# Position attention, linear attention and sorted experts on one core: sorted rows turned by loads and VectorE, and four changes of order

## The chip, the core and the metric

The kernel runs on one core of a Trainium2 chip. A core has five engines that run their own instruction streams in order and wait for each other through semaphores: TensorE (PE in the profile; PEld is its loading of weights), VectorE (DVE), ScalarE (ACT), GpSimd (POOL) and SyncE (SP), which here only issues DMAs. Sixteen DMA engines move data between the chip's memory (DRAM) and the core's buffers. The metric is the time of one execution on the device, in microseconds (us), as the median of several runs. The profile is of one such execution; its span runs from the first to the last instruction.

## What is computed

The input is `x`, 4 images of 32 channels of 128 x 128 values in fp32. Two layers follow each other, image by image:

```
# layer 0: attention over the positions of 2x2 patches
q      = x as [128 (channel, r, s), 4096 positions] of an image       # 64 x 64 positions
energy[i, j] = (q[:, i] . q[:, j]) / (|q[:, i]| |q[:, j]|)            # 4096 x 4096
x      = gamma * (sum over j of softmax_j(energy)[i, j] * q[:, j]) + q

# layer 1: 4096 tokens t of 128 values (the rows of x)
t = t + linear attention(LayerNorm(t))          # 8 heads, K^T V first, then Q (K^T V)
p = softmax(LayerNorm(t) @ router_w + router_b) # 8 experts
t = t + sum over the two likeliest experts e of  p_e / (p_1 + p_2) * (LayerNorm(t) @ W_e + b_e)
```

The bulk of the work is the 4096 x 4096 energy of layer 0, cut into 8 chunks of 512 positions. It is symmetric before the softmax's division, so that a tile of exponents serves two rows of chunks.

## The kernel before

**Layer 0, `attend`.** Row `i` of 8 has the tiles `jc = 0..i`, each of four *steps* `j`. A step issues one product `pe` (line 609), its exponential `pr` on ACT (L612), and what is due from two queues. `turn_tick` (L416) runs what was queued with `after(ticks, f)`: two steps after a `pr`, its product `po` with the values (L497); one step after it, the turn of `pr` into `F` in 32 x 32 blocks on DVE (L421 in the profile, a helper's line). When a tile's four `pr` are turned, `move` stores `F` to DRAM (`blocks<-F`, L530), and three steps later `bring` loads the blocks back in exchanged places (`F<-blocks`, L545, six DMAs). This is an *F exchange*; `F` then holds the tile transposed and is used for row `jc`. That use is a *share*: four products `pg` (L433, or L453 for the diagonal tile), each with a sum on ACT (L438) and at the end an addition on DVE (L442). A share is put in the list `late` with a due time; `step_share` (L468) does one quarter of the first share in the list, if its due time has come by a counted clock:

```python
late.append((at or clock[0] + LAG, transposed_share(b, st, i, jc, G)))   # LAG = 57
```

A full step adds 8 to the clock and a quarter of a share adds 4. When row `i` has had its last `po`, ACT copies the bank out (`o<-po`, L502). There is one such bank, so the next row's first `po`, at the third step (`j == 2`) of its first tile, needs that copy.

**What runs beside it.** PE, DVE, ACT and SP follow the order in which the Python code calls them (a manual schedule); GpSimd has an order of its own. Besides `attend` of image `b` there are generators that are advanced between steps: `prep` loads and scales the next image's chunks (quarters of rows in `xa`, turned by DVE into `qT`, L316; squares and sums, L295 and L296; the power -1/2 on GpSimd, L164; `wide`, L388; `pnorm` on PE, L399), and the layer 1 of the image before (`all_parts`), one advance (`yield`) in each half of a step. For image 0 `prep_first` makes the first pair of chunks and `prep(0, 1)` the second, each with 512 KB of quarters in one and the same buffer (`xin`, tag `xx`).

**Layer 1.** `close_rows` divides, normalises and forms a Gram matrix; `matrix` folds the heads; `attention_rows(u)` for each quarter of the tokens fetches normalised rows in 128-byte pieces (`blocks<-rows`, L938), adds the attention, takes statistics (`close_stats`, whose power runs on GpSimd) and normalises again on ACT (L696). After every second quarter `sorted_experts(h)` handles half of the tokens (`h` = 0, 1). It sorts by expert: GpSimd scatters each token's row twice to `xs` in DRAM (L1066), in tiles of 128 rows that belong to one expert, 39 tiles for a half. Each row is 132 values long, 128 of the token and its weight in the rest. Then, for pairs of tiles, SP loads them (`xn<-xs`, L1096), PE turns each tile with the identity (L1137), ACT evicts the turned pair (L1106), PE multiplies each tile by its expert's matrix (L1130), DVE multiplies by the weights while it evicts (`results<-pys`, L1112), and SP stores the pair (`ys<-results`, L1116). Last, GpSimd gathers each token's two rows (L1178). Images 0 to 2 do this; the last image's experts are done densely at the end (L1304).

Of the kernel before, what the change touches and what calls it, by code (L numbers as in the profile page):

```python
# [12 lines left out]
F32 = mybir.dt.float32  # L13
# [9 lines left out]
def kernel(  # L23
# [43 lines left out]
    nc = tc.nc  # L67
# [231 lines left out]
        rows = st["T"][:, ts(kc, 8), :]  # L299
        return rows.rearrange("p k (w r) -> p k w r", r=2)  # L300

    def load_quarters(b, kc, queues=(nc.sync, nc.sync)):

        xa = xin.tile([P, 2, 2, 2, HW2, 2], F32, tag="xx", name=f"xa_{b}_{kc}")
# [7 lines left out]
        return xa  # L312

    def turn_quarters(s, xa, qT):
        for k in range(2):
            nc.vector.transpose(  # L316
                qT[:, s, 2 * k : 2 * k + 2, :].rearrange("p h (e r c) -> p r (h e) c", e=2, r=2),
                xa[:, s, k].rearrange("p r (h t) e -> p (r h) e t", h=2),
            )

    def prep_first(st):

        b, kc = 0, 0
        st["T"] = big1.tile([P, KT, D], F32, tag="T", name="T_0")
        xa = load_quarters(b, kc, (nc.sync, nc.scalar))
        qT = chunks_of(b, kc, st)
        yield
        ss = stat.tile([P, 2 * NJ], F32, tag="ss", name=f"ss_{b}_{kc}")
        rn = stat.tile([P, 2 * NJ, 1], F32, tag="rn", name=f"rn_{b}_{kc}")
        for s in range(2):  # L330
            turn_quarters(s, xa, qT)
            squares(b, kc, s, qT, ss)
            pow_neg_half(rn[:, ts(s, NJ), 0], ss[:, ts(s, NJ)])
        keep_running(40, ps_g, "pg")
        scaled = []
        for s in range(2):
            qs = work.tile([P, NJ, P], F32, tag="qs", name=f"qs_{b}_{kc}_{s}", bufs=2)
            nc.vector.tensor_tensor(qs, qT[:, s], rn[:, ts(s, NJ)].to_broadcast([P, NJ, P]), ALU.mult)
            scaled.append(qs)
        for s, qs in enumerate(scaled):  # L340
            qn = channels(b, kc, s, st)
            pt, done = hold(f"ptn_{b}_{kc}_{s}", lambda p, qn=qn: nc.scalar.activation(qn, p, AF.Copy))  # L342
            for j in range(NJ):
                nc.tensor.transpose(pt[:, ts(j, P)], qs[:, j, :], ident)
            done()
            yield

    def prep(b, kc, st):

        ahead = 2 if b == 0 and kc == 1 else 5
        xa = load_quarters(b, kc)
# [3 lines left out]
        for _ in range(ahead):  # L357
            yield
        qT = chunks_of(b, kc, st)
        for s in range(2):  # L360
# [17 lines left out]
        rn = stat.tile([P, 2 * NJ, 1], F32, tag="rn", name=f"rn_{b}_{kc}")  # L378
        for s in range(2):
            squares(b, kc, s, qT, ss)  # L380
            if s == 1:
                pow_neg_half(rn[:, :, 0], ss)
            yield
        for _ in range(ahead - 2):
            yield
        wide = work.tile([P, NJ, 2, 64], F32, tag="qs", name=f"wide_{b}_{kc}", bufs=2)
        for s in range(2):
            nc.vector.tensor_copy(wide[:, :, s], rn[:, ts(s, NJ)].to_broadcast([P, NJ, 64]))  # L388
        yield
        if b:  # L390
            yield

        def scale_all(bank):
            for s in range(2):
                scale(s, bank, lambda ap: ap.rearrange("p (j a t) -> p a j t", a=4, t=S))

        bank, done = hold(f"pnorm_{b}_{kc}", scale_all)
        for j in range(NJ):
            nc.tensor.transpose(bank[:, ts(j, P)], wide[:, j].rearrange("p s c -> p (s c)"), ident)  # L399
        yield  # L400
        done()
        yield
# [71 lines left out]
    def attend(b, st):  # L474
# [11 lines left out]
        for i in range(NCH):  # L486
# [94 lines left out]
            for jc in order:  # L581
# [21 lines left out]
                for j in range(NJ):  # L603
                    t = NJ * jc + j
                    c0 = 0 if jc < i else P * j
                    yield
                    tick[0] += 1
                    pe = ps_e.tile([P, CH], F32, tag="pe", name=f"pe_{b}_{i}_{t}")
                    nc.tensor.matmul(pe[:, c0:], qn[jc][:, ts(j, P)], qn[i][:, c0:], start=True, stop=True)  # L609
                    pr = ppool.tile([P, CH], F32, tag="pr", name=f"pr_{b}_{i}_{t}")  # L610
                    exps[:] = [
                        nc.scalar.activation(pr[:, c0:], pe[:, c0:], AF.Exp, accum_out=sums[:, t, i : i + 1]).ins  # L612
                    ]
                    own.append(pr)
                    if ending and jc == order[-1] and j == NJ - 1:
                        st["exps"] = True
                    after(2, partial(values, pr[:, c0:], t, c0, CH))
                    if jc < i and not both:
                        after(1, partial(nc.vector.transpose, Fb[:, :, :, j, :], pr))
                        if j == NJ - 1:  # L620
                            after(2, partial(move, F, i, jc))
                    elif jc == i and not ending:
                        if j < NJ - 1:
                            after(1, partial(turn_blocks, F, pr, j))
                        if j == NJ - 2:
                            after(2, partial(move_diagonal, F, i))
                    elif jc == i and j in (1, 2):

                        after(1 if j == 2 and order[-1] == i else 2, partial(below, own, (2, 1) if j == 1 else (3,)))
                    turn_tick()  # L630
                    clock[0] += 2 * (CH - c0) // P
                    step_share()
                    yield

    def finish():
# [18 lines left out]
    def layer1(b, st):  # L654
# [288 lines left out]
        def attention_rows(u):  # L943
# [17 lines left out]
            for j in range(8):  # L961
                stats[j]()
                if j == 3:
                    yield
                    yield
            logits = router_rows(nc.vector, 8 * u, 8, la)
            close_stats("f", 8 * u, 8, bs)
            next(logits)
            yield
            nc.sync.dma_start(t2[:, ts(u, 8)], T[:, ts(u, 8), :])  # L970
            yield
# [15 lines left out]
        def sorted_experts(h):  # L987
# [112 lines left out]
            def products(turned, applied):  # L1100
# [36 lines left out]
                        nc.tensor.transpose(p[:, ts(j, P)], bufs[g % 6][:, j, :D], ident)  # L1137
                return done

            if "results" not in keep:  # L1140
                keep["results"] = work.tile([P, 4, 2, D], F32, tag="df", name=f"results_{b}", bufs=1)
            done = None
            begins = []
            for at in range(len(pairs) + 5):
                if at < len(pairs):
                    load(*pairs[at])
                if done:
                    done()
                yield
                turned, applied = (pairs[at - d] if 0 <= at - d < len(pairs) else None for d in (3, 4))  # L1150
                done = products(turned, applied) if turned or applied else None
                yield
            if done:
                done()
            if h == 1:
                st["sorted"] = True
            yield from idle(1)
# [271 lines left out]
    for b in range(B):  # L1429

        if b == 0:
# [80 lines left out]
```

## Time and profile before

| | us |
|---|---|
| median of 3 runs | 1651.85 (1651.45 to 1653.72) |
| the profiled execution | 1650.83 |
| its span | 1649.0 |

| group | count | busy us | mean ns |
|---|---|---|---|
| L1137 PE pys<-ident,xn, transposes of sorted tiles | 234 | 45.2 | 273 |
| L1130 PE pys<-ew_sb,xn, their products | 468 | 71.6 | 275 |
| L1106 ACT xn<-pys, eviction of a turned pair | 120 | 45.2 | 377 |
| L1112 DVE results<-pys,xn, 128x256 | 114 | 48.2 | 423 |
| L421 DVE F<-pr, turn of 128x512 | 440 | 305.4 | 700 |
| L938 SP blocks<-rows, DMA issue | 48 | | 744 (median) |

Matmuls overlap, so that a PE group's mean is longer than the time for which one holds PE. A product in fp32 has two records, a transpose one. Letters before the arrow name what is written, those after it what is read. "Idle before" is the engine's idle time just ahead of a group, with what ended it.

### The profile page before, as it was taken

Reading aid. Unit: us, or ns where it says so; the run is one execution under the profiler, and the core shown is the slowest. Engines: PE = TensorE matmul, PEld = TensorE weight load, DVE = VectorE, ACT = ScalarE, POOL = GpSimd, SP = SyncE. Lnnn points to the kernel's source line nnn. Section 1 sums busy time; section 2 is a strip of 40 time slices with the busy share of each in tenths; the row PEclk is TensorE's granted clock in tenths of the full one; section 3 lists DMA queues with packets and bytes.
Section 4 is the critical chain, followed back from the end, with each engine's and each line's share of the span. In section 5 each row is a group of like instructions: output and inputs, shape, how many; then the busy total and the mean of one; then the engine's idle time right before and its main releaser. Section 6 shows DMA issues by size and latency. Waiting matters only on the chain.

```text
span 1649.0 us, 21309 instructions
## 1 busy us (share of the span) xinstructions
PE 1609.9 (98%) x5192; PEld 846.5 (51%) x5192; DVE 931.5 (56%) x2383; ACT 898.5 (54%) x2839; POOL 593.8 (36%) x565
## 2 busy tenths in 40 slices
PE   8999999999999999999999999999999999999987
PEld 4444544455554455555554455555554455555633
DVE  4543353567586443549478443448658634345786
ACT  3555445466475555547556455556656555545386
POOL 1000000001015441446555543256555652437166
PEclk9999999999999999999999999999999999999999
DMA  4655656676759777997899777798699877886001
GB/s 143 205 179 178 197 187 213 222 231 204 168 196 283 239 222 220 266 257 200 211 221 287 253 236 241 222 268 230 196 209 279 275 248 236 248 251 192 14 14 39
DMA packets 304297, 345.37 MB, mean 209 GB/s; under 512 B 82096, under 2 KB 230704, under 8 KB 289840
## 3 DMA queue, kind: packets, MB, share of 16 engines
q1 hardware_dynamic: 269712, 304.50, 59.9%
q0 software_dynamic: 26624, 25.58, 7.6%
q10 hardware_dynamic: 7840, 13.93, 2.9%
q8 instruction: 44, 0.72, 0.2%
q14 instruction: 77, 0.63, 0.1%
HBM read 167.08 MB, written 182.09 MB: 212 GB/s over the span
## 4 chain that ended last, share of the span: by engine, by line
PE 81%; DVE 7%; DMA 5%; ACT 3%; SPq 2%; issue 1%; POOL 1%; ACTq 0%; DVEq 0%; POOLq 0%
PE po L497 24%; PE pe L609 23%; PE pg L433 20%; PE pys L1130 3%; PE py L1304 3%; PE pg L453 2%; PE pys L1137 2%; PE pgram L725 2%; DMA F<-blocks 1%; DVE F L421 1%; DMA blocks<-rows 1%; SPq L938 1%; ACT pr L612 1%; ACT xn L696 1%; DMA blocks<-F 1%
## 5 line engine op out<-in xcount | busy, mean ns | idle before, releaser
L612 ACT ACTIVATE pr<-pe 128x512 f32<-128x512 f32 (+1 forms) x576 | 322.4, 560 | 547.5 <-PE pe L609 507.0
L497 PE MATMUL po<-pr,qT 128*128 128x512 f32 (+3 forms) x1152 | 549.4, 559 | 4.2 <-ACT o L502 3.9
L609 PE MATMUL pe<-qn,qn 128*128 128x512 f32 x896 | 458.8, 594 | 4.6 <-ACT pr L612 4.6
L433 PE MATMUL pg<-F,qT 128*128 128x512 f32 x880 | 449.8, 593 | 4.7 <-DMA F<-blocks 4.7
L421 DVE STREAM_TRANSPOSE F<-pr 128x512 f32<-128x512 f32 x440 | 305.4, 700 | 134.5 <-ACT pr L612 124.7
L497 PEld LDWEIGHTS po<-pr,qT 128*128 128x128 f32 x1152 | 215.2, 190 | 250.2 <-issue 217.9
L1178 POOL DMA_INDIRECT acc<-ys,place x128 | 202.1, 1579 | 209.1 <-ACT pr L612 134.8
L438 ACT ACTIVATE junk<-F 128x512 bf16<-128x512 f32 x440 | 273.0, 620 | 4.9 <-DMA F<-blocks 4.9
L433 PEld LDWEIGHTS pg<-F,qT 128*128 128x128 f32 x880 | 166.8, 190 | 199.4 <-issue 182.3
L1066 POOL DMA_INDIRECT xs<-xn,place x192 | 186.0, 969 | 184.1 <-ACT pr L612 118.9
L609 PEld LDWEIGHTS pe<-qn,qn 128*128 128x128 f32 x896 | 155.6, 191 | 119.1 <-issue 106.7
L442 DVE TENSOR_TENSOR o<-o,pg 128x512 f32<-128x512 f32 x110 | 75.1, 683 | 205.4 <-PE pg L433 205.2
L1112 DVE TENSOR_TENSOR results<-pys,xn 128x256 f32<-128x256 f32 x120 | 49.9, 416 | 187.2 <-ACT xn L1106 168.5
L164 POOL TENSOR_TENSOR rn<-ss,neg_half 128x8 f32<-128x8 f32 (+1 forms) x17 | 27.2, 1602 | 320.0 <-DVE ss L296 319.9
L612 ACT ACTIVATION_READ_ACCUMULATOR pr<-pe 128x1 f32 x576 | 111.9, 194 | 0.0
L1106 ACT ACTIVATE xn<-pys 128x256 f32<-128x256 f32 x120 | 45.2, 377 | 111.4 <-PE pys L1137 111.4
L1130 PEld LDWEIGHTS pys<-ew_sb,xn 128*128 128x128 f32 x468 | 70.5, 191 | 52.2 <-issue 49.7
L609 PE MATMUL pe<-qn 128*128 128x512 f32 (+3 forms) x256 | 91.4, 440 | 0.7 <-ACT qn L342 0.7
L1178 POOL DMA_INDIRECT yb<-ys,place x64 | 60.8, 950 | 81.1 <-DMA F<-blocks 31.1
L438 ACT ACTIVATION_READ_ACCUMULATOR junk<-F 128x1 f32 x440 | 84.5, 192 | 0.0
L1130 PE MATMUL pys<-ew_sb,xn 128*128 x468 | 71.6, 275 | 0.0
L1304 PE MATMUL py<-ew_sb,xn 128*128 128x512 f32 x128 | 61.5, 622 | 5.1 <-ACT tmp L1260 3.9
(217 smaller groups left out, 1463.2 us busy)
## 6 DMA issues: line engine op xcount, KB each, us to landing
blocks<-F SPq DMA_DIRECT2D x110, 1024.0 KB
F<-blocks SPq DMA_DIRECT2D x220, 192.0 KB
F<-blocks SPq DMA_DIRECT2D x220, 128.0 KB
xn<-xs SPq DMA_DIRECT2D x114, 132.0 KB
ys<-results SPq DMA_DIRECT2D x114, 128.0 KB
F<-blocks SPq DMA_DIRECT2D x220, 64.0 KB
below<-F SPq DMA_DIRECT2D x31, 384.0 KB
T<-in_x_dram SPq DMA_DIRECT2D x64, 128.0 KB
```

The costliest lines, as they stand in the source:

```text
L421: f()
L433: nc.tensor.matmul(pg.rearrange("p (a f) -> p a f", a=4), st["qT"][i][:, ib, :], G[:, :, ib], start=(ib == 0), stop=(ib == NJ - 1),)
L438: nc.scalar.activation(junk, G[:, :, ib], AF.Copy, accum_out=st["sums"][:, NJ * i + ib, jc : jc + 1])
L442: nc.vector.tensor_tensor(st["o"][jc], st["o"][jc], pg, ALU.add)
L497: nc.tensor.matmul(row["po"][:, lo:hi], qT[blk // NJ][:, blk % NJ, :], w, start=start, stop=(row["left"] == 0))
L609: nc.tensor.matmul(pe[:, c0:], qn[jc][:, ts(j, P)], qn[i][:, c0:], start=True, stop=True)
L612: nc.scalar.activation(pr[:, c0:], pe[:, c0:], AF.Exp, accum_out=sums[:, t, i : i + 1]).ins
L1066: inst = nc.gpsimd.indirect_dma_start(xs[h], offset(place[:, i, k : k + 1]), xn[:, k, :], None)
L1112: nc.vector.tensor_tensor(result[:, :n], p[:, 2 * P : 2 * P + n * D].rearrange("p (j c) -> p j c", c=D), bufs[g % 6][:, :n, D : D + 1].to_ ...
L1130: nc.tensor.matmul(p[:, 2 * P + j * D : 2 * P + j * D + D], bufs[6 + g % 2][:, j, :D], weights[:, bass.ds(begins[2 * (g % 2) + j], D)], st ...
L1178: inst = nc.gpsimd.indirect_dma_start(to, None, ys, offset(place[:, i, k : k + 1]), compute_op=op)
L1304: nc.tensor.matmul(bank, xn[:, k, :D], ew_sb[:, 4 * h : 4 * h + 4, :], start=True, stop=True)
```

## The change

Five things change.

1. In the first half (`h == 0`) of an image's sorted rows, TensorE no longer turns the tiles. Four loads for each group of up to four tiles bring 32 x 32 blocks, in rows of 128 bytes, to the places where a turn of blocks alone completes the transpose; DVE turns 128 x 512 at once; PE multiplies four tiles into one bank, and one eviction and one store serve four tiles. The weights of all rows come by one load of their own (`factor`, 39 values for each of 128 partitions). The second half stays as it was.
2. At the start of image 0, the second pair's quarters have a buffer of their own and are loaded right after the first pair's; their four turns stand between the first pair's operations on DVE.
3. In a step that is the third of a row's first tile, `step_share` comes ahead of `turn_tick`. In all steps the clock is advanced ahead of both.
4. `attention_rows` has three more `yield`s: before the logits and the statistics' end, after them, and before the store of `t2`.
5. `prep` of image 0 has one `yield` more before `pnorm`, as the other images have.

```diff
+        def rows_squared(s):
             turn_quarters(s, xa, qT)
-            squares(b, kc, s, qT, ss)
+            sq = work.tile([P, NJ, P], F32, tag="qs", name=f"sq_{b}_{kc}_{s}", bufs=2)
+            nc.vector.tensor_tensor(sq, qT[:, s], qT[:, s], ALU.mult)
+            return sq
...
+        summed(0, rows_squared(0))
+        sq = rows_squared(1)
+        st["turns"].pop(0)()
+        scale_rows(0)
+        summed(1, sq)
+        st["turns"].pop(0)()
+        st["turns"].pop(0)()
+        scale_rows(1)
+        st["turns"].pop(0)()
...
+        soon = b == 0 and kc == 1
+        if soon:
+            xa = load_quarters(b, kc, place=(work, "wide"))
+            yield
...
+        if soon:
+            st["turns"] = [partial(turn_quarter, s, k, xa, qT) for s in range(2) for k in range(2)]
+            yield
...
-        if b:
-            yield
+        yield
...
-                    turn_tick()
                     clock[0] += 2 * (CH - c0) // P
-                    step_share()
+                    steps = (turn_tick, step_share)
+                    for step in reversed(steps) if jc == order[0] and j == 2 else steps:
+                        step()
                     yield
...
+            yield
             logits = router_rows(nc.vector, 8 * u, 8, la)
             close_stats("f", 8 * u, 8, bs)
+            yield
             next(logits)
+            yield
             yield
             nc.sync.dma_start(t2[:, ts(u, 8)], T[:, ts(u, 8), :])
...
+            def load_blocks(g, n):
+                rows = xs[h][4 * g * P : (4 * g + n) * P, :D].rearrange("(m i) w -> i m w", i=S)
+                for q in range(4):
+                    read(
+                        nc.sync.dma_start(
+                            parts[g % 2][ts(q, S), : n * D].rearrange("i (m c) -> i m c", c=S), rows[:, :, ts(q, S)]
+                        )
+                    )
+
+            def turn(g, n):
+                nc.vector.transpose(parts[2 + g % 2][:, : n * D], parts[g % 2][:, : n * D])
+
+            def four_products(factor, g, n):
+
+                def leave(p):
+                    result = keep["results"].rearrange("p g j c -> p (g j) c")[:, ts(g % 2, 4)]
+                    nc.vector.tensor_tensor(
+                        result[:, :n], p[:, : n * D].rearrange("p (j c) -> p j c", c=D),
+                        factor[:, 4 * g : 4 * g + n].to_broadcast([P, n, D]), ALU.mult,
+                    )
+                    nc.sync.dma_start(
+                        ys[4 * g * P : (4 * g + n) * P, :].rearrange("(j p) d -> p j d", p=P), result[:, :n]
+                    )
...
+            def turned_by_vector():
+
+                factor = stat.tile([P, NT, 1], F32, tag="factor", name=f"factor_{b}_{h}", bufs=1)
+                read(nc.sync.dma_start(factor, xs[h].rearrange("(t p) w -> p t w", p=P)[:, :, D : D + 1]))
+                leaves = {}
+                for at in range(4 * len(quads) + 10):
+                    for first_at, act in (
+                        (8, turn), (0, load_blocks), (11, partial(four_products, factor)), (13, lambda g, n: leaves.pop(g)()),
+                    ):
+                        if at >= first_at and (at - first_at) % 4 == 0 and (at - first_at) // 4 < len(quads):
...
+            yield from (turned_by_tensor if h else turned_by_vector)()
...
     next(first)
-    load_weights()
-    next(first)
     next(second)
+    load_weights()
+    ordered.enter_context(tc.manual_schedule(engines=ENGINES))
+    next(second)
+    next(first)
     load_tokens(states[0]["T"][:, 0:8, :], 0, 0, 8)
-
-    ordered = ExitStack()
-    ordered.enter_context(tc.manual_schedule(engines=ENGINES))
-    timed = [(first, 0, 1, 2), (second, 0.5, 5.5, 10)]
+    next(second)
+    next(second)
+    timed = [(first, 0, 1, 2), (second, 1.3, 5.5, 8)]
```

More of the change, by code (lines that the diff above doesn't have):

```diff
@@ L300, in rows_of_image, with load_quarters @@
         return rows.rearrange("p k (w r) -> p k w r", r=2)
-    def load_quarters(b, kc, queues=(nc.sync, nc.sync)):
-        xa = xin.tile([P, 2, 2, 2, HW2, 2], F32, tag="xx", name=f"xa_{b}_{kc}")
+    def load_quarters(b, kc, queues=(nc.sync, nc.sync), place=(xin, "xx")):
+        xa = place[0].tile([P, 2, 2, 2, HW2, 2], F32, tag=place[1], name=f"xa_{b}_{kc}")
         halves = x[b].rearrange("c (s g) w -> c s (g w)", s=2)
@@ L312, in load_quarters, with turn_quarter @@
         return xa
+    def turn_quarter(s, k, xa, qT):
+        nc.vector.transpose(
+            qT[:, s, 2 * k : 2 * k + 2, :].rearrange("p h (e r c) -> p r (h e) c", e=2, r=2),
+            xa[:, s, k].rearrange("p r (h t) e -> p (r h) e t", h=2),
+        )
     def turn_quarters(s, xa, qT):
         for k in range(2):
[L316 to L319, printed above, removed]
+            turn_quarter(s, k, xa, qT)
     def prep_first(st):
@@ L329, in prep_first, with summed, scale_rows @@
         rn = stat.tile([P, 2 * NJ, 1], F32, tag="rn", name=f"rn_{b}_{kc}")
-        for s in range(2):
+        def rows_squared(s):
             turn_quarters(s, xa, qT)
-            squares(b, kc, s, qT, ss)
+            sq = work.tile([P, NJ, P], F32, tag="qs", name=f"sq_{b}_{kc}_{s}", bufs=2)
+            nc.vector.tensor_tensor(sq, qT[:, s], qT[:, s], ALU.mult)
+            return sq
+        def summed(s, sq):
+            nc.vector.tensor_reduce(ss[:, ts(s, NJ)], sq, AX.X, ALU.add)
             pow_neg_half(rn[:, ts(s, NJ), 0], ss[:, ts(s, NJ)])
[L334 to L337, printed above, removed]
+        def scale_rows(s):
+            qs = work.tile([P, NJ, P], F32, tag="grp", name=f"qs_{b}_{kc}_{s}", bufs=2)
             nc.vector.tensor_tensor(qs, qT[:, s], rn[:, ts(s, NJ)].to_broadcast([P, NJ, P]), ALU.mult)
             scaled.append(qs)
+        scaled = []
+        keep_running(40, ps_g, "pg")
+        summed(0, rows_squared(0))
[7 more added lines that the diff above has]
+        st["turns"].pop(0)()
         for s, qs in enumerate(scaled):
@@ L348, in prep @@
     def prep(b, kc, st):
-        ahead = 2 if b == 0 and kc == 1 else 5
-        xa = load_quarters(b, kc)
+        soon = b == 0 and kc == 1
+        ahead = 2 if soon else 5
+        if soon:
+            xa = load_quarters(b, kc, place=(work, "wide"))
+            yield
+        else:
+            xa = load_quarters(b, kc)
         if b == 0:
@@ L356, in prep @@
             xx = rows_of_image(b, kc, st)
-        for _ in range(ahead):
+        qT = chunks_of(b, kc, st)
+        if soon:
+            st["turns"] = [partial(turn_quarter, s, k, xa, qT) for s in range(2) for k in range(2)]
             yield
-        qT = chunks_of(b, kc, st)
-        for s in range(2):
+        for _ in range(0 if soon else ahead):
+            yield
+        for s in range(0 if soon else 2):
             turn_quarters(s, xa, qT)
@@ L1138, in products, with read @@
                 return done
+            room = xn[:, half, :].rearrange("p k w -> p (k w)")
+            parts = [room[:, 4 * DW * i : 4 * DW * i + 4 * D] for i in range(4)]
+            quads = [(g, min(4, NT - 4 * g)) for g in range((NT + 3) // 4)]
+            def read(inst):
+                wait_for(inst.ins, xs_made[h], "a tile holds tokens of any row")
+                xs_read[h].append(inst.ins)
+            def load_blocks(g, n):
[6 more added lines that the diff above has]
+                    )
@@ new lines, in turn @@
+            def turn(g, n):
[9 more added lines that the diff above has]
+                        ys[4 * g * P : (4 * g + n) * P, :].rearrange("(j p) d -> p j d", p=P), result[:, :n]
+                    )
+                p, done = hold(f"pys_{b}_{h}_{g}", leave)
+                _, begins = nc.values_load_multi_w_load_instructions(
+                    begin[0:1, h, 4 * g : 4 * g + n], engines=[mybir.EngineType.PE], min_val=0,
+                    max_val=(E - 1) * D,
+                    skip_runtime_bounds_check_because="D times a count of at most E - 1, never negative",
+                )
+                weights = ew_sb.rearrange("p e c -> p (e c)")
+                for j in range(n):
+                    nc.tensor.matmul(
+                        p[:, ts(j, D)], parts[2 + g % 2][:, ts(j, D)],
+                        weights[:, bass.ds(begins[j], D)], start=True, stop=True,
+                    )
+                return done
@@ new lines, in turned_by_vector @@
+            def turned_by_vector():
[7 more added lines that the diff above has]
+                        if at >= first_at and (at - first_at) % 4 == 0 and (at - first_at) // 4 < len(quads):
+                            g, n = quads[(at - first_at) // 4]
+                            made = act(g, n)
+                            if first_at == 11:
+                                leaves[g] = made
+                    yield
@@ L1140, in sorted_experts, with turned_by_tensor @@
             if "results" not in keep:
                 keep["results"] = work.tile([P, 4, 2, D], F32, tag="df", name=f"results_{b}", bufs=1)
-            done = None
             begins = []
-            for at in range(len(pairs) + 5):
-                if at < len(pairs):
-                    load(*pairs[at])
+            def turned_by_tensor():
+                done = None
+                for at in range(len(pairs) + 5):
+                    if at < len(pairs):
+                        load(*pairs[at])
+                    if done:
+                        done()
+                    yield
+                    turned, applied = (pairs[at - d] if 0 <= at - d < len(pairs) else None for d in (3, 4))
+                    done = products(turned, applied) if turned or applied else None
+                    yield
@@ L1147, in sorted_experts @@
                 if done:
                     done()
[L1149 to L1154, printed above, removed]
+            yield from (turned_by_tensor if h else turned_by_vector)()
             if h == 1:
@@ L1419 @@
     first, second = prep_first(states[0]), prep(0, 1, states[0])
-    next(first)
-    load_weights()
+    ordered = ExitStack()
     next(first)
     next(second)
+    load_weights()
+    ordered.enter_context(tc.manual_schedule(engines=ENGINES))
+    next(second)
+    next(first)
     load_tokens(states[0]["T"][:, 0:8, :], 0, 0, 8)
-    ordered = ExitStack()
-    ordered.enter_context(tc.manual_schedule(engines=ENGINES))
-    timed = [(first, 0, 1, 2), (second, 0.5, 5.5, 10)]
+    next(second)
+    next(second)
+    timed = [(first, 0, 1, 2), (second, 1.3, 5.5, 8)]
     for b in range(B):
```

## The prediction

> **What bounds the kernel now.** I read the page's busy times first, then who TensorE waited for, then single stretches of the timeline around each wait that the change touches.
>
> ```profile
> PE 1609.9 (98%) x5192; PEld 846.5 (51%) x5192; DVE 931.5 (56%) x2383; ACT 898.5 (54%) x2839; POOL 593.8 (36%) x565
> ...
> PE pg L433 <- DMA F<-blocks: 4.7, 3, 1.9
> PE pe L609 <- ACT pr L612: 4.6, 3, 1.6
> PE py L1304 <- ACT tmp L1260: 3.9, 4, 2.5
> PE po L497 <- ACT o L502: 3.9, 16, 0.5
> PE pnorm L399 <- DVE wide L388: 2.6, 2, 2.4
> PE ptn L344 <- DVE qs L338: 2.6, 1, 2.6
> ...
> 571.00:645.00 74.00, 73.82 (x262) 40.32 (x261) 32.28 (x61) 38.70 (x121) 28.81 (x30) 1.00 0.76 233
> ```
>
> TensorE (PE) is busy for 1609.9 of 1649.0 us, so only 39 us of the span are not its own work. In the waits, the columns are total us, number of waits and the longest. The last line is the stretch in which image 0's first half of sorted rows is multiplied: PE has no room in it, while VectorE (DVE) and ScalarE (ACT) are half idle. A PE instruction taken out here shortens the span one for one, as long as nothing new makes PE wait.
>
> **What the Trainium skill says.** "VectorE: DVE Perf Modes", section "The three transpose paths": TensorE turns a whole 128x128 into PSUM, VectorE only 32x32 blocks, within SBUF. So blocks have to be put in their places by the loads. The trace has such a turn already: 128x512 on VectorE takes 700 ns (L421), 692 ns in L950. "DMA: Bandwidth & Descriptors", "Rules for kernel authors": a strided last dimension becomes one descriptor per element. The new load of 39x128 single factors is such a case; no row here shows one. The same page, "Queues, rings and completion order": each engine takes descriptors in ring order. The trace agrees, see the fetch below. "Perfetto Trace Analysis", "What "DMA-bound" means": a DMA issue's profiled window is descriptor generation, not data movement.
>
> **The change, part by part.**
>
> *1. Turning without TensorE.* An image's first half has 39 tiles, three images have it: 3 x 39 = 117 of the 234 transposes of L1137 go. What one costs PE is read from starts, since matmuls overlap:
>
> ```profile
> 620.75 0.61 PE L1130 MATMUL pys<-ew_sb,xn 128*128 x4
> 621.20 0.38 PE L1137 MATMUL pys<-ident,xn 128*128 128x128 f32 x2
> 621.41 1.02 PE L609 MATMUL pe<-qn,qn 128*128 128x512 f32 x2
> ```
>
> Two transposes hold PE from 621.20 to 621.41: 0.107 us each, weight loads included. 117 x 0.107 = **12.5 us** off PE. The products (L1130) stay, 234 of them. ACT loses 60 evictions of 377 ns, 22.6 us, which hides behind PE.
> DVE gains per four tiles one turn (700 ns by L421) and swaps two evictions of 423 ns for one of 128x512 (about 690 ns, by L1213): 700 + 690 - 846 = 0.54 us, 30 times = 16 us. A group of four takes two steps, about 5.8 us; DVE's work in it is two F turns (1.4), half an add (0.34), and 1.39 new: 3.1 us. It fits; cost 0.
> DMAs: four loads of 32x16 pieces of 128 bytes replace two of 528-byte rows. SyncE's issue of a 1024-piece fetch (L938) lasts 557 ns at best and 744 ns in the middle; I take 0.55 us for 512 pieces. Per group SyncE then spends 4 x 0.55 + 0.43 (store) = 2.6 us, against 1.7 before, and 1.5 us for its share of an F exchange: 4.1 of 5.8 us. It still fits. What SyncE is queued with behind these loads are the F exchanges (1 MB out, six loads back), and TensorE waits for those. What such loads can do stands in the attention stage of image 1:
>
> ```profile
> 834.59 0.61 SPq L530 DMA_DIRECT2D blocks<-F  x1
> 835.30 4.87 SPq L938 DMA_DIRECT2D blocks<-rows  x4
> 840.26 7.88 SPq L545 DMA_DIRECT2D F<-blocks  x6
> ...
> 850.92 1.10 PE L433 MATMUL pg<-F,qT 128*128 128x512 f32 x2 [1.79 <-DMA F<-blocks]
> ```
>
> Two fetches of 4096 pieces within 11 us (829.7 to 840.2) held an exchange so that PE waited 1.79 us. The new loads bring 2048 pieces in 5.8 us, half that rate, and their turn runs eight yields (four steps, some 11 us) later. The factor load is once per image: 4992 elements, by the fetch's worst issue rate (3385 ns for 1024) up to 16 us, at its best rate (557 ns) 2.7 us; I take 5. Behind it stands the exchange of the diagonal tile, issued at 572.0 now and used by PE (L453) at 595.9: 10 us late would still do. The first turn may keep DVE 2 to 3 us for its data; the next store of results held SyncE from 579 to 588 anyhow. I take 0.5 us of PE wait per image, **1.5 us** in all; bounds 0 and 15.
>
> *2. Image 0's start.* Now the second pair's blocks are loaded only after the first has left its buffer, and turned at 15.3 to 17.3; PE waits for the result:
>
> ```profile
> 9.74 0.69 DVE L338 TENSOR_TENSOR qs<-qT,rn 128x512 f32<-128x512 f32 x1 [0.94 <-POOL rn L164]
> 10.35 0.68 DVE L296 TENSOR_REDUCE ss<-sq 128x4 f32<-128x512 f32 x1
> 12.15 0.69 DVE L338 TENSOR_TENSOR qs<-qT,rn 128x512 f32<-128x512 f32 x1 [1.12 <-POOL rn L164]
> ...
> 21.95 0.49 DVE L388 COPY wide<-rn 128x256 f32<-128x256 f32 x2 [1.13 <-POOL rn L164]
> ```
>
> In the new order DVE fills the two waits for GpSimd's power (0.94 and 1.12 us) with turns of the second pair, 0.34 us each. From 5.62: two turns to 6.3, square to 6.9, sum to 7.5, two turns to 8.2, square to 8.8, a turn of the second pair to 9.2, scaling at 9.2 instead of 9.74. The second pair's 512 KB are issued from about 2.1 on; the first 512 KB took until 5.42, so I expect them by 9. After scaling, the second pair's squares and sums (2.7 us) and power (1.6) end near 17, the copies near 18, ahead of the place where PE now waits until 22.50. The 2.39 us go. If the second load slows the first, ptn comes later by as much: bounds 1.5 and 3.0. I take **2.4**. The first half of 2.64 us before ptn stays.
>
> *3. Share first in a row's first tile.* Meant is the wait of a row's first product for the eviction of the row before (L502): 16 waits, 3.9 us. But the clock is now advanced ahead of the turn of the queue, so a share's due time, clock + 57, is counted from a value 8 higher. In the changed program's order, at the third step of rows 0 and 3 to 7 no share is due yet: the row's first product still stands right behind its pe, and the share follows a step later. Only rows 1 and 2 of images 1 to 3 have it first, and none of the waits lies there (415.72, for instance, is row 3). I take **0**, bounds -0.2 and 1.
>
> The same 8 units have another effect: a share comes a step later, 1.7 us at least (a pe and a po of 0.86 each). The waits for F (1.00 at 184, 1.79 at 851, 1.87 at 1240) are of this size. 4.7 us go but for some 0.1 to 0.2 each: **4.2**, bounds 2 and 4.7. An F buffer is held a step longer; it is begun again 24 steps later, by the sixth tile after, and is free after about 18 (4 to fill, 4 to go out and be called back, 5 or 6 of lag, 4 to be used), so that costs nothing.
>
> *4. Attention stage drawn apart.* Once per image ACT stands still for GpSimd's factors before it normalises, and PE waits for an exponent behind it:
>
> ```profile
> 485.37 1.65 ACT L696 ACTIVATE xn<-T,nbo,rsf 128x128 f32<-128x128 f32 x4 [3.77 <-POOL nbo L692]
> ```
>
> That ACT wait of 3.77 us gave 1.51 us of PE wait at 487.64; 1.56 at 876 and 1265. Between the statistics' end and the normalising two yields (a step) become four. One more step of 2.6 us leaves ACT about 1.2 us, which PE's two banks cover. **4.6 us** go, bounds 3 and 4.6. The stage ends 3 yields later, but in the changed program's order image 2's second half of sorted rows ends two steps earlier, counted from the end, and its last combination moved from 1537 to ahead of the division at 1529.7, where its data (landed near 1526) are there. The last 160 instructions of PE are the same. Cost 0.
>
> Sum: 12.5 + 2.4 + 0 + 4.2 + 4.6 - 1.5 = 22.2 us. The profiled execution took 1650.83 us around a span of 1649.0; it becomes about 1628.6. The median of the runs lies 1.0 us above the profiled one (1651.85): I forecast **1629.5 us**.
>
> **Rivals.** *The first half gives its gain back*: factor load, pieces and the turn in DVE's fixed order cost PE about 4 us in each of three images, 12.5 in all: 1642 (1636 to 1646). For it speaks that SyncE is 70% issued there and DMA at 0.76 before the pieces; against it, that the scatter stage, 495 to 515, runs at a DMA share of 1.04 with one PE wait of 0.18 us. *The later share and the drawn-out stage move the waits instead of ending them*: 8.8 us stay, 1638. For it: DVE is without a gap from 476 to 491, so statistics may run late again. *Slower*: the pieces hold every F exchange of that stage. There are six exchanges per image, 18; gains without the 1.5 are 23.7 us, so it decides from 1.3 us of PE wait per exchange. At 1.8, the wait of 850.92, the loss is 32.4: 1660. Against it stands the halved rate and the share's extra step. *Part 3 does not do what it says*: this is in the forecast; were it to work, 3.7 us more go: 1626.
>
> **How the numbers follow.** Forecast 0.65 (its own range 1625 to 1634), gain given back 0.13, waits moved 0.08, slower 0.07, part 3 at work 0.05, no change 0.02. The range 1624 to 1643 leaves out the slower case and the tails. Faster by over 0.2% (3.3 us, about what can be told apart): 0.91; within 0.2%: 0.02; slower: 0.07.
>
> **What would show it.** L1137's group at 117; PE busy near 1597; no wait of pnorm at the start; waits "po <- ACT o" still near 3.9 us; "pe <- ACT pr" and "pg <- DMA F<-blocks" nearly gone; turns of xn at 700 ns. Wrong it would be if PE shows gaps in the three stretches of the first half, or if SyncE's issue of the factor load takes over 10 us with F behind it.

## The result and the profile after

The changed kernel takes 1647.78 us (median of 22 runs, 1646.11 to 1651.72), the kernel before 1651.28 us beside it (22 runs): 0.9982 of it, 95% interval 0.9974 to 0.9990. The gain is 3.0 us by the ratio. Forecast were 22 us.

The page's busy times and TensorE's waits of the changed kernel (total us, number, longest):

```profile
PE 1609.3 (98%) x5075; PEld 827.2 (50%) x5075; DVE 939.0 (57%) x2383; ACT 871.6 (53%) x2779; POOL 592.3 (36%) x565
...
PE po L523 <- ACT o L528: 4.6, 20, 0.5
PE pbd L798 <- DVE rdx L776: 3.9, 5, 1.5
PE pys L1167 <- DMA xn<-xs: 3.3, 2, 1.7
PE ptn L363 <- DVE qs L345: 2.3, 1, 2.3
PE py L1401 <- ACT tmp L1357: 2.2, 4, 0.8
PE pg L459 <- DMA F<-blocks: 2.1, 1, 2.1
```

The 117 instructions are gone (5192 before, 5075 here). The waits of `pnorm` and of `pe` for `pr` are gone. One is new, that of `pbd` for `rdx` (`rdx` holds the factors of the softmax's division, made by DVE in `close_rows`; `pbd` is PE's transpose of them), and the one for `xn<-xs` grew from 0.7 us before to 3.3. Yet PE is as busy as before, 1609.3 against 1609.9 us, with 12.5 us of work taken out. So other instructions of PE last longer, without a wait that this view would count. It is in the groups, where the columns after the count are busy us, mean ns of one, and the idle time ahead with what ended it:

```profile
L1160 PE MATMUL pys<-ew_sb,xn 128*128 x234 | 41.6, 299 | 1.4 <-ACT xn L1136 1.1
L1210 PE MATMUL pys<-ew_sb,xn 128*128 x234 | 31.1, 275 | 0.4 <-DVE xn L1188 0.4
L1160 PEld LDWEIGHTS pys<-ew_sb,xn 128*128 128x128 f32 x234 | 30.8, 190 | 43.7 <-ACT xn L1136 42.7 <-issue 1.0
```

L1210 are the products of the first half, the one that was changed: 275 ns, as before. L1160 are those of the second half, whose code was not changed: 299 ns. The last line is their weight loads. They sat idle for 42.7 us until ACT had evicted the turned tile that is to be loaded. The same group of the kernel before:

```profile
L1130 PEld LDWEIGHTS pys<-ew_sb,xn 128*128 128x128 f32 x468 | 70.5, 191 | 52.2 <-issue 49.7 <-ACT junk L438 1.0
```

There no wait for an eviction is named. What that costs is seen in one pair of tiles, first in the changed kernel, then before (timeline: start, duration, engine, line):

```profile
664.19 0.19 ACT L464 ACTIVATION_READ_ACCUMULATOR junk<-F 128x1 f32 x1
664.29 0.37 ACT L1136 ACTIVATE xn<-pys 128x256 f32<-128x256 f32 x1
...
664.71 0.71 PE L1160 MATMUL pys<-ew_sb,xn 128*128 x4
```

```profile
664.88 0.19 PEld L1130 LDWEIGHTS pys<-ew_sb,xn 128*128 128x128 f32 x1 [0.24 <-issue]
...
665.31 0.61 PE L1130 MATMUL pys<-ew_sb,xn 128*128 x4
...
666.17 0.38 ACT L1106 ACTIVATE xn<-pys 128x256 f32<-128x256 f32 x1 [1.08 <-PE pys L1137]
```

Before, the eviction (666.17) follows its transposes at once and is ready about a step ahead of the products that read it; their first weight load runs at 664.88, while the share's last product (`pg`) still streams. Now the eviction is called after the step's exponent and the share's sum (`junk`), ends at 664.66, and the products read it at 664.71. The first product starts 0.54 us after the start of the share's last product instead of 0.43, and holds PE 0.21 us instead of 0.11: 0.21 us for a pair, and no idle time of PE is shown for it.

Why the eviction moved: a step of `attend` has two halves, and the layer-1 generators advance once in each. The loop for the second half of the tokens transposes a pair in one half of a step and evicts it in the next. Part 4 added three yields to each `attention_rows(u)`, in whose generator the sorted experts run. Three is odd, so everything behind them in the generator changed to the other half of a step. Which half it falls in is called the phase below.

The time from an instruction's start to the next start on PE ("start to start" below), less what it is where nothing waits, was summed over the trace by what came next. From before to after it changed by:

| | forecast us | trace us |
|---|---|---|
| transposes | -12.5 | -12.7 |
| first half's loads and turns | +1.5 | +0.6 |
| `pnorm`, `ptn` at the start | -2.4 | -3.2 |
| F | -4.2 | -2.8 |
| `po` for `o` | 0 | +0.9 |
| `pbd` for `rdx` | none | +5.0 |
| `pe` for `pr` | -4.6 | -5.1 |
| second half's products | none | +13.4 |
| second half's first loads (`xn<-xs`) | none | +2.7 |
| last stage (differs from run to run) | 0 | -1.3 |

The sum is -2.5; the span went from 1649.0 to 1646.3. The forecast column sums to -22.2. Of the 19.7 us between them, 16.1 are the second half's products and first loads, and 5.0 are `rdx`.

### The profile page after: what moved, and what is told of

Its sections match the earlier page's. It is cut to its first block, busy times and chain, and to the rows that moved or that the text cites. A ratio compares the mean times of both kernels' runs of the same rounds, so it can differ in the third digit from the quotient of the medians.

```text
span 1646.3 us, 20939 instructions
## 1 busy us (share of the span) xinstructions
PE 1609.3 (98%) x5075; PEld 827.2 (50%) x5075; DVE 939.0 (57%) x2383; ACT 871.6 (53%) x2779; POOL 592.3 (36%) x565
## 4 chain that ended last, share of the span: by engine, by line
PE 85%; DVE 6%; DMA 4%; ACT 2%; SPq 1%; issue 1%; POOL 0%; ACTq 0%; DVEq 0%
PE po L523 25%; PE pe L635 24%; PE pg L459 21%; PE py L1401 3%; PE pys L1160 2%; PE pg L479 2%; PE pgram L752 2%; PE pys L1210 2%; PE pat L882 2%; DMA blocks<-F 1%; DVE df L785 1%; PE pys L1167 1%; DVE bs_a L810 1%; SPq L571 1%; DMA xn<-xs 1%
## 5 line engine op out<-in xcount | busy, mean ns | idle before, releaser
L164 POOL TENSOR_TENSOR rsa<-dm_a,neg_half 128x8 f32<-128x8 f32 x16 | 26.5, 1655 | 120.5 <-DVE sv_a L715 120.5
L1142 DVE TENSOR_TENSOR results<-pys,xn 128x256 f32<-128x256 f32 (+1 forms) x60 | 24.8, 413 | 75.3 <-ACT xn L1136 68.6
L635 PEld LDWEIGHTS pe<-qn 128*128 128x128 f32 x256 | 45.3, 192 | 37.6 <-issue 32.4
L164 POOL TENSOR_TENSOR rsf<-dm_f,neg_half 128x8 f32<-128x8 f32 (+1 forms) x15 | 26.3, 1754 | 99.0 <-DVE sv_f L715 99.0
```

Of the source, the lines that this page charges most:

```text
L164: pinned(nc.gpsimd.tensor_tensor(dst, src, neg_half.to_broadcast(list(src.shape)), ALU.pow))
```

## The experiments

All are given as a ratio to the kernel before on the same chip, with 95% intervals. The chips differ: the kernel before takes 1651.7 us on the one of e9 to e12, and 1661.6 to 1662.2 us on the others.

| run | kernel | ratio |
|---|---|---|
| e1 | changed, phase restored | 0.9960 (0.9946 to 0.9973) |
| e2 | part 1 alone | 0.9893 (0.9877 to 0.9909) |
| e3 | part 3 alone | 1.0065 (1.0051 to 1.0080) |
| e4 | parts 1, 2, 3 | 0.9960 (0.9945 to 0.9974) |
| e5 | changed | 1.0000 (0.9991 to 1.0009) |
| e6 | parts 1, 2 | 0.9890 (0.9876 to 0.9905) |
| e7 | parts 1, 2, share first, old clock | 0.9850 (0.9833 to 0.9868) |
| e8 | before, phase shifted in the first half | 1.0114 (1.0099 to 1.0129) |
| e9 | e7, statistics closed sooner | 0.9829 (0.9817 to 0.9842) |
| e11 | parts 1, 2, clock early | 0.9962 (0.9948 to 0.9977) |
| e12 | changed, two yields for three | 0.9962 (0.9948 to 0.9976) |
| e13 | part 1 alone | 0.9917 (0.9897 to 0.9938) |
| e14 | parts 1, 2 | 0.9883 (0.9865 to 0.9901) |
| e15 | changed | 0.9988 (0.9978 to 0.9997) |
| e16 | changed, phase restored | 0.9962 (0.9947 to 0.9977) |

### The phase (e1, e5, e15, e16, e12, e8)

```diff
+            if h:
+                yield
             yield from (turned_by_tensor if h else turned_by_vector)()
```

> The changed kernel with one more yield ahead of the second half's loop, nothing else. Theory A (phase): the attention stage's three added yields per group are an odd number, so the second half's turned tiles are now evicted in the other half of a step, right before the products that read them, and each pair of tiles costs TensorE 0.21 us more (products L1160 152 ns from start to start on average, 113 before; 58 pairs): with the yield the first product of a pair follows the share by 0.43 instead of 0.54 us, the group is near 113 ns again, and the time falls by 11 to 12 us, to about 1636. Rival B (traffic): the evictions are late because the new loads and turns of the first half have filled ACT's and DVE's queues: the yield changes nothing that counts, 1646 to 1649.

> The changed kernel once more, as the control for the kernel with the phase restored (0.996 of the kernel before, where the change had measured 0.9982 elsewhere). Theory A (phase): restoring it is worth the 0.21 us at each of some 57 pairs, 11 to 12 us, so here the changed kernel is 0.7% behind it, 1.002 to 1.004 of the kernel before. Rival: the waits that show beside the phase take most of that back when it is restored: 0.997 to 0.999.

These two ran on different chips, so both were run once more on one:

> The changed kernel on the same chip as the phase restored. Against parts 1 and 2: part 3's clock 11 us and part 4's phase 12 us, less 4.6 us for the waits of pe: 0.9975 to 1.000 of the kernel before.

> The phase restored, on the same chip as the changed kernel. Theory A: 0.21 us at 57 pairs, of which new waits for rdx and counts (some 4 us) take a part: 0.4 to 0.7% under the changed kernel. Rival: what the two chips showed (0.996 and 1.000) was the chips' difference: 0.1% or less.

The second half's groups in e16:

```profile
L1160 PE MATMUL pys<-ew_sb,xn 128*128 x234 | 35.8, 274 | 0.0
L1160 PEld LDWEIGHTS pys<-ew_sb,xn 128*128 128x128 f32 x234 | 35.2, 191 | 26.1 <-issue 25.4
```

The wait for the eviction is gone, products last 274 ns again. From start to start they take 119 ns on average, against 149 in e15. Traced against each other, e15 and e16 agree within 0.22 us until the first image's second half; e16 then gains 6.1 us in that half, 6.1 us in the next image's and 2.5 in the last one's. In between it gives 2.7 back to waits for `rdx` and for the run counts (`pcnt`), and leads by 11.7 us at 1446. Then a stop of all engines, of which below, takes 4.3, and 6.8 us at half the granted TensorE clock, which begin in it, take some 3 more; the spans differ by 6.9 us. By the ratios the phase is worth 0.26% in time (0.9988 to 0.9962), less than the 0.4% to 0.7% expected, and 0.4% between e5 and e1, which lay between the two theories' numbers. The intervals of e15 and e16 leave room for 0.1% to 0.4%. The granted clock may have a part in it: its median is 0.992 in the six runs of e16 and 0.995 in the 22 of e15, by an estimate 5 us (0.003 of 1656). Whether that comes with the restored phase is open. The 11 to 12 us of e1 were right for PE's work and too high for the time.

e12 takes one of the three yields out again, so that the number is even:

```diff
             next(logits)
             yield
-            yield
```

> The changed kernel with two of part 4's three added yields, an even number. Theory A (phase): the second half's products follow their shares by 0.43 us again (group near 115 ns from start to start, 152 in the changed kernel), the pe waits in the attention stage mostly stay away; 0.4 to 0.7% under the changed kernel, 0.993 to 0.996 of the kernel before. Rival: what counts is how long the stage is, not whether the number is odd: products near 150 ns, 0.999 to 1.001.

The group is at 115 ns from start to start, and the weight loads wait for ACT no more:

```profile
L1159 PEld LDWEIGHTS pys<-ew_sb,xn 128*128 128x128 f32 x234 | 35.3, 191 | 26.6 <-issue 25.6 <-ACT junk L464 0.2
```

The time is 0.9962, against 0.9982 for three yields, both where the kernel before takes 1651 us; the two intervals just touch. The group and its weight loads decide between the theories: that the number is odd is what counts. Most of the gain in `pe` waits stays (1.9 us of waiting), but `rdx` rises to 7.5 us.

e8 shifts the phase of the kernel before, in its first half alone:

```diff
             done = None
             begins = []
+            if not h:
+                yield
             for at in range(len(pairs) + 5):
```

> The kernel before with one yield ahead of the loop of the first half only, nothing else: the phase alone, on the other half. Theory A: each of the first half's some 58 pairs costs TensorE 0.21 us more (the first product of a pair follows the share by 0.54 instead of 0.43 us and holds 0.21 instead of 0.11 us): 12 us, 1.007 of the kernel before; L1131's group goes from 113 to about 130 ns from start to start. Rival: the yield moves nothing that TensorE waits for: 1.000 +- 0.001.

```profile
L1130 PEld LDWEIGHTS pys<-ew_sb,xn 128*128 128x128 f32 x468 | 66.4, 190 | 68.3 <-ACT xn L1106 36.5 <-issue 29.1 <-ACT junk L457 1.1
```

The wait is made with one yield: 36.5 us, at 47 pairs, 47 x 0.21 = 9.9 us. From the start of the instruction ahead of each group to the end of its last product, start to start, the products take 12.2 us longer than in the first trace of before, near the 12 expected. The time rose by more, 1.14% or 19 us. Some 3 us of it are longer waits for F (7.8 us in all, 4.7 in the first trace of before). The two longest of these, 3.7 and 3.0 us, are each followed by 3.4 us at half the granted clock, at 858.1 and 1254.0, which the first trace of before does not have there: up to 1.7 us each. That comes near the 19 us; as the two traces are of different chips, it is no proof.

### The clock (e3, e4, e6, e14, e11)

e2, e3, e4 and e6 are the change's own parts, put into the kernel before.

> The kernel before with the share order and the earlier clock alone (part 3). As predicted for the step: the waits for F (4.7 us) go, nothing else: 1647. Theory A now: the F waits of 851 and 1240 go (3.7 us) but the one near 184 grows by 1.1 us, and shares that come a step later put VectorE's sums before the division late (waits of pbd for rdx, 3.9 us in the changed kernel): 1650 to 1652. Rival: the rdx waits belong to the drawn-out stage or to part 2: no pbd wait here, 1647 to 1648.

> The changed kernel with the attention stage not drawn apart (parts 1, 2 and 3 only). Theory A: the second half's phase is the old one, so 11 to 12 us come back and the three waits of pe for pr (4.6 us) return: about 1640. Rival B: 1650 to 1653, slower than the changed kernel by the 4.6 us alone.

> Parts 1 and 2 alone: the kernel before with the first half's turning and image 0's earlier second pair, shares and attention stage as before. By the prediction's terms 12.5 - 1.5 + 2.4: 13.4 us faster than before. By what part 1 alone measured (0.9893) and 2.4 us for part 2: 0.987 to 0.989 of the kernel before. Rival: part 2 lengthens the start elsewhere (its load stands ahead of the weights') and gives nothing: 0.989 to 0.991; the wait of pnorm near 21 us is gone in either case.

> Parts 1 and 2 once more, beside part 1 alone on the same chip. If part 2 is worth the 2.5 us wait of pnorm: 0.0015 under part 1 alone. Rival: no difference, as the two measured apart (0.9893 and 0.989).

Part 3 alone costs 0.65%, nearly 11 us, more than either theory had, where 4.2 us of gain were forecast; its trace has 6.1 us of `pbd` waits for `rdx`. Beside parts 1 and 2 it costs the same (0.9890 to 0.9960). In e4 the second half's products take 126 ns, so most of the phase was back, as expected. But the 1640 expected, beside 1651.3 of the kernel before, would be 0.993: 5 us are missing, for a reason that neither theory had. e11 takes the clock without the order:

```diff
-                    turn_tick()
                     clock[0] += 2 * (CH - c0) // P
+                    turn_tick()
                     step_share()
```

> Parts 1 and 2 with the clock advanced ahead of the queue in every tile, and no share moved ahead of the queue: part 3's clock without part 3's order. If the clock is what part 3 costs: as slow as parts 1 to 3 together, 0.995 to 0.998 of the kernel before, with rdx waits of 4 to 6 us and pe waits of 8 to 10. Rival: it is the share first in rows 1 and 2 that costs: 0.988 to 0.990, as parts 1 and 2.

```profile
PE pe L635 <- ACT pr L638: 8.1, 6, 2.4
PE pbd L797 <- DVE rdx L775: 5.9, 5, 1.7
```

It is the counted clock. Up to 1304 us of e6, ahead of that chip's stops, e11 is 13.8 us late: 6.8 by `pbd`, none of which e6 has, 4.5 by `pe` behind a share, 1.1 by the second half's loads. These sums hold more than waits. Behind e11's longest waits TensorE was granted half its clock for 3.4 us (two lines of a timeline, then the stretch, with the granted clock third from the end):

```profile
1260.41 1.02 PE L523 MATMUL po<-pr,qT 128*128 128x512 f32 x2
...
1264.69 2.08 PE L635 MATMUL pe<-qn,qn 128*128 128x512 f32 x2 [2.40 <-ACT pr L638]
```

```profile
1264.70:1268.10 3.40, 3.40 (x4) 1.50 (x5) 3.04 (x9) 3.40 (x11) 0.00 (x0) 0.50 0.74 254
```

Two products take 2.08 us there instead of 1.02. In the stretch compared, e11 has three of these (at 182.7, 875.6 and 1264.7, behind waits of 2.3, 2.3 and 2.4 us) and e6 none after its first 16 us: up to 5 of the 13.8 us. How `rdx` comes to be late is seen on DVE, before and then in the changed kernel:

```profile
387.52 0.23 DVE L744 TENSOR_REDUCE den<-sums 128x8 f32<-128x72 f32 x1
387.78 0.20 DVE L745 RECIPROCAL rd<-den 128x8 f32<-128x8 f32 x1
388.02 0.62 DVE L749 TENSOR_SCALAR rdx<-rd,gam 128x256 f32<-128x256 f32 x2
388.55 1.30 DVE L421 STREAM_TRANSPOSE F<-pr 128x512 f32<-128x512 f32 x2
389.88 0.55 DVE L462 TENSOR_TENSOR o<-o,pg 128x384 f32<-128x384 f32 x1
```

```profile
386.08 0.87 DVE L810 BATCH_NORM_STATS2 bs_a<-T 128x6 f32<-128x128 f32 x4
...
387.84 0.70 DVE L447 STREAM_TRANSPOSE F<-pr 128x512 f32<-128x512 f32 x1
388.57 0.56 DVE L488 TENSOR_TENSOR o<-o,pg 128x384 f32<-128x384 f32 x1
389.04 0.22 DVE L771 TENSOR_REDUCE den<-sums 128x8 f32<-128x72 f32 x1
389.30 0.20 DVE L772 RECIPROCAL rd<-den 128x8 f32<-128x8 f32 x1
389.54 0.65 DVE L776 TENSOR_SCALAR rdx<-rd,gam 128x256 f32<-128x256 f32 x2
```

`close_rows` begins when two rows have all their shares. With shares called a step later it begins elsewhere in DVE's order: the sums stand behind another group's statistics, a turn and a share's addition, and `rdx` is ready some 1.5 us later than before, while PE reaches `pbd` at nearly the same point (390.25 after a wait of 0.81; 389.43 before). e11, which has no part 4, shows the same order and the same wait of 0.81 us. That the waits of `pe` grow for the same reason was not shown separately.

### The order without the clock, and the best kernel (e7, e9)

```diff
-                    turn_tick()
+                    first = jc == order[0] and j == 2
+                    if not first:
+                        turn_tick()
                     clock[0] += 2 * (CH - c0) // P
                     step_share()
+                    if first:
+                        turn_tick()
```

> Parts 1 and 2 with the share ahead of the queue in a row's first tile and the clock advanced where it was (after the queue in every other tile). If the share's order is what part 3 gains and the early clock what it costs: the waits of po for ACT's o fall from 3.7 us to under 1, no rdx waits, and 2 to 4 us less than parts 1 and 2 alone. Rival: the order itself delays what hangs on the share: po waits gone but pe or pbd waits in their place, no gain.

```profile
PE pg L459 <- DMA F<-blocks: 5.3, 3, 2.4
...
PE po L523 <- ACT o L528: 0.2, 1, 0.2
```

The waits of `po` are gone (3.7 us in e6). From row to row the trace is some 0.45 us shorter where a wait had been counted at 0.18. Up to 1304 us of e6 that makes 8.6 us, of which later shares' waits for F, called sooner now, take 2.6 back. The ratio says 0.4%, 6.6 us, above the 2 to 4 expected.

e9 keeps e7 and draws the attention stage apart without a yield more:

```diff
             for j in range(8):
                 stats[j]()
-                if j == 3:
-                    yield
-                    yield
             logits = router_rows(nc.vector, 8 * u, 8, la)
             close_stats("f", 8 * u, 8, bs)
+            yield
             next(logits)
             yield
+            yield
```

> Parts 1 and 2, the share first with the old clock, and the attention stage drawn apart without added yields: the two yields amid a group's statistics stand behind their end instead, so the statistics close two yields sooner before the normalising and every later phase is kept. Theory: the waits of pe for pr near 482, 865 and 1248 (1.5 us each, 4.6 in all) go and nothing else changes: 0.3% under the share-first kernel, 0.982 of the kernel before. Rival: VectorE's eight statistics in one piece hold the turns of F and PE waits there instead: 0.985 to 0.987.

Page and waits of e9:

```profile
PE 1595.2 (98%) x5075; PEld 835.3 (51%) x5075; DVE 942.9 (58%) x2383; ACT 878.1 (54%) x2779; POOL 596.3 (37%) x565
...
PE pg L459 <- DMA F<-blocks: 5.0, 3, 2.4
PE py L1400 <- ACT tmp L1356: 3.9, 4, 2.5
PE ptn L363 <- DVE qs L345: 2.1, 1, 2.1
```

No `pe` waits for `pr`, and the products are at 112 ns. 1624.28 us, 0.9829: the best of all, with the four aims of the change met and its two side effects avoided. On its chip the kernel before was traced too:

> The kernel before itself, for its trace on the chip of these runs. If the stops seen near 1310 to 1335 and 1490 to 1530 in all the other kernels' traces belong to the chip and the place in the program and not to a kernel, this one has them too (some 1 to 5 us each), and its span is 1655 or more. If they come with the first half's new loads: none here, a span near 1650.

Its span was 1648.5 us, with no stop in it, as in no trace of this chip, so that the run could not tell whether the kernel before has them elsewhere. Here the two traces can be compared in full: the span fell by 26.0 us to 1622.5.

### Part 1 (e2, e13)

> The kernel before with the first half's turning alone (part 1). Theory A: part 1 delivers what it was costed at, 117 transposes of 0.107 us, and nothing takes it back: 1638 to 1640, no longer waits in the second half, its products near 113 ns from start to start. Rival B: part 1 itself gives the gain back (loads, SyncE, the second half starting late): 1646 to 1651, with product waits in the second half as in the changed kernel.

> Part 1 alone once more, on the same chip as the next three. If part 1 is worth its transposes, 117 times 0.108 us from start to start, and the rest of the first measurement (0.9893, 17.8 us) was that chip's stops: 0.9915 to 0.993 of the kernel before where no trace shows stops, 0.989 again where they do. If part 1 gives more than the transposes: 0.989 in either case, with PE waits gone that the trace can name.

Part 1 keeps its gain: 0.9893 on one chip, 0.9917 on another, 18 and 14 us, where its transposes are worth 12.7. Whether the few us above that are the chips' stops stays open, as neither chip has a trace of before. e14 on e13's chip is 0.34% lower with part 2, e6 and e2 on two chips showed 0.03%; part 2's trace says 2.9 us, within both intervals.

## Why the prediction was wrong

*Part 1* was right. 12.5 us were forecast, 12.7 came. The 1.5 us for the new DMAs were hardly needed: in three first halves PE waits once for a turn, 0.4 us (L1210 above; 0.6 from start to start). In image 0's it has no gap, with the DMA share up from 0.76 to 0.90 (the columns are the stretch, PE, PEld, DVE, ACT, GpSimd busy, clock, DMA share, GB/s),

```profile
571.00:645.00 74.00, 74.00 (x244) 39.06 (x243) 36.01 (x63) 33.33 (x107) 26.91 (x29) 1.00 0.90 240
```

and the factor load, put at 5 us of SyncE, has an issue of 388 ns (L1219, 382 to 394). The Trainium skill's "DMA: Bandwidth & Descriptors", "Rules for kernel authors", which was taken as a reason for a long issue, counts descriptors; for 4992 single values here the issue was shorter than for the 1024 pieces of L938, 557 ns at best. The turns of 128x512 took 697 ns (700 forecast).

*Part 2* was right: 2.4 us, 2.9 with the later pairs' `pnorm`.

*Part 3* was wrong in its counted clock. That the share would not be first, so that the `po` waits stay, was right (4.6 us). The forecast then took the later share as a gain for F, at no cost: "a share comes a step later ... 4.2". F gave 2.8, because the wait near 183 us grew from 1.0 to 2.1 while those at 851 and 1240 went. The step that failed is the cost of the later share, put at nothing without asking who waits for a share. `close_rows` does, and then DVE and `pbd`: the clock alone costs some 12 us (e11 beside e6, 0.9962 to 0.9890), in the changed kernel at least the 5.0 us at `pbd`. The rival that part 3 works was put at 3.7 us, the sum of its waits; the order alone gave 0.4%, 0.45 us at each row.

*Part 4* was right in its wait (4.6 forecast, 5.1 gone from start to start) and wrong in "The stage ends 3 yields later ... Cost 0". Only the distance was counted, not the parity. The three yields moved the second half's evictions to the other half of the step: +13.4 us on its products and +2.7 on its first loads, and so took back all of part 1's gain, in a place that the change does not touch. e16, e12 and e8 show this mechanism.

Of the rivals, "the first half gives its gain back" had nearly the size of this loss (12.5 us) by coincidence, for it put it in the wrong half and on other causes; "waits moved" named part 3 and 4, but no wait that came. Among the signs named ahead, "PE busy near 1597" failed clearly, with 1609.3, and it pointed to the cause; the waits for F, to be nearly gone, kept 2.1 of 4.7 us. The Trainium skill, "Perfetto Trace Analysis", "Identifying the Most-Contended Engine", warns that matmul busy time is not a good measure of how close a kernel is to its limit, since pipelined instructions look smaller in the trace. Here it misled the other way: a product whose weight load was late looked larger, 377 ns instead of 275, and counted as busy.

## What to carry to other kernels

Where generators are advanced at fixed points of a loop, count the yields that an edit adds modulo the loop's points, and look at what lies behind it in the same generator: the distance from producer to consumer can fall from about a step to nothing. Before a step is made later, list everything that waits for it, also the conditions in the Python code that start another stage. When instructions go and busy time does not, sum start to start by group, and look at the weight loads' waits as well as the matmuls', and at the granted clock behind PE's longest waits.

## What the runs showed of the hardware

A weight load that waits for its data cost PE in two places here: 0.11 us ahead of the first product and 0.10 us more in it (377 ns instead of 275), although PE shows no idle time. An idle time of 0.18 us before a row's first `po` stood for some 0.45 us from row to row.

A long wait of PE can cost more than its length. The traces of all runs have 29 stretches before 1500 us in which half the TensorE clock was granted, of 3.4 us each, in three cases 6.8. Each begins during a PE wait of 1.9 us or more, or at most 2.0 us after its end. In such stretches of e15 and e16 a product of 128x512 mostly held PE for 853 ns instead of 429, so that 3.4 us cost up to 1.7. Not every long wait has one behind it: 19 waits of 2.0 us or more have none, the 2.11 us at 180.6 of the changed kernel among them.

On three of the four chips of the experiments each trace has one or more stops between 1308 and 1345 us or 1489 and 1529 us (one to five us each) in which PE, ACT and DVE all stand, whatever the kernel, though the kernel before was not traced there; on the chip of e9 to e12 and in the first two traces there is none there. In e15 (timeline):

```profile
1328.75 0.59 PE L459 MATMUL pg<-F,qT 128*128 128x512 f32 x1
...
1332.16 0.60 ACT L638 ACTIVATE pr<-pe 128x512 f32<-128x512 f32 x1 [5.10 <-remote]
1332.22 0.69 DVE L468 TENSOR_TENSOR o<-o,pg 128x512 f32<-128x512 f32 x1 [5.03 <-remote]
...
1332.90 1.12 PE L635 MATMUL pe<-qn,qn 128*128 128x512 f32 x2 [3.56 <-ACT pr L638]
```

ACT and DVE resume within 0.06 us of each other, PE behind them. The cause was not found.
